# Two value products moved in the hand-written order of a two-layer graph-network kernel

## The chip, the cores and the metric

The kernel runs on one core of a Trainium2 chip. The metric is the device time of one execution in microseconds (us), as the median of several runs. A profile is one further execution, recorded by the hardware; its own time is given beside it. Engines are called by the profile's names: PE is the matmul engine and PEld its weight loads, DVE the vector engine, ACT the scalar engine, POOL the general engine, SP the engine that only issues DMAs here.

## The reference, cut to what matters

128 graphs of 128 nodes with 256 features each pass through two layers. The first is an attention layer whose attention matrix is split by edge type (four types, of which the adjacency here uses 0 and 1), followed by a norm, a feed-forward net with GELU and a second norm. The second consists of two graph attentions in a row, a norm, a feed-forward net with ReLU and a last norm.

```python
# layer 0
q, k = src @ Wq + bq, src @ Wk + bk                 # 8 heads of 32
attn = softmax(q k^T / sqrt(32))
out = sum over r of (attn * (adj == r)) @ (src @ Wv[r] + bv[r])
x = ln(src + out @ Wo + bo, g1, beta1)              # norm 0
x = ln(x + gelu(x @ W1 + b1) @ W2 + b2, g2, beta2)  # norm 1
# layer 1
h = gat(gat(x, adj, W1, a1), adj, W2, a2)
h = ln(x + h, g_ln1, b_ln1)                         # norm 2, "the graph norm"
x = ln(h + relu(h @ w_ff1 + b_ff1) @ w_ff2 + b_ff2, g_ln2, b_ln2)   # norm 3
```

All of it is float32. W1, W2, w_ff1 and w_ff2 are 256 x 1024 and 1024 x 256.

## The kernel before, in words

**Tiling.** The 16384 rows (128 graphs of 128 nodes) are worked in 32 groups of T = 512 rows, four graphs each. For each group the kernel keeps x (rows on partitions), xT (features on partitions) and the transposed adjacency. A second pass for general adjacencies exists behind a flag that the first pass computes; it doesn't run on these inputs.

**Steps as generators.** The work of a group is cut into Python generators, each `yield` being the end of a step: `projections` (two steps for q, two for k, then four for v, one for each block of 128 rows), `attention`, `norm`, `ffn`, `layer1`. The function `in_order` takes a list of such generators and calls the next step of each in the order of the list, with `(f2, 2)` for two steps in a row. That list, written by hand, fixes the order in which instructions stand in each engine's queue; nothing reorders them later. Waits between engines follow from the tiles that they share.

**The steady order.** From group 1 on (`g` in the loop over groups) one pass of the loop holds three groups at different stages: the first feed-forward net of S1 = group g + 1 (`f1`), the second one of S = group g (`f2`), the two graph attentions (`l1`), and the projections (`pr`), attention (`at`) and norm 0 of S2 = group g + 2. Two `in_order` lists make up the pass. The first ends in the transposes of S for its second feed-forward net (`turned(S, 2)`), the first half of the attention of S2 and the end of `f1`; the second begins with `f2`. `pr` has eight steps in the pass: four for q and k early in the first list, and four value products `pv` (L570), one for each block, around the point where the lists meet. Each value product is two 128x512 matmuls into one buffer of the PSUM pool `ps_s` (tag "s", four buffers in rotation, shared with score tiles, transposes and most other products), after which DVE adds the bias row into `v` (L574). In what follows they are called pv 0 to pv 3, and their sums v 0 to v 3. v 0 and v 1 are read by the first half of the attention, v 2 and v 3 by the second. The pass with g = 0 and the last ones have orders of their own, or no S2 left.

**The transposes.** `turned(S, 2)` transposes the four normalised blocks of x on PE (L290, tile `pt`, two tiles of four transposes), evicts them on ACT with the norm's scale and bias (L293, tile `yT`), and makes four sums of halves of yT on DVE (L378 to L381, tile `yS`). The blocks are normalised by ACT (L338, four instructions), which waits for a small DVE row `sh` (L333), which in turn waits for a power on POOL (L325), which waits for a DVE row (L324).

**The feed-forward nets.** Each is computed by a scheme of seven products of half-sized blocks instead of eight (Winograd's form of Strassen's). For each of four parts r of the hidden layer these products follow each other on PE (L400):

- P1, the form B11 with a11 (first step, `begun(0)`), into the bank `fa`; ACT copies it to the bank `seeded` (L438);
- P7, the form T3 with s3, into the bank `fe`; ACT copies it to `p7` (L445);
- the form T2 with s2, added into `seeded`; ACT copies the sum to `p16` (L449);
- B21 with a12, added into `fa`, then the activation on ACT (L424);
- T1 with s1, added into `seeded`; DVE adds p7 to the sum (L455), and ACT activates;
- T4 with a22, added into `fe`; DVE adds p16 (L459);
- P1 of the next part, and B22 with s4.

A second set of seven products (L409) makes the output.

**Around the change.** `n1` is the norm 1 of S1. It has been given its root (L324 and L325) at the end of the first list; its step in the second list is the normalisation itself (`sh` on DVE, four L338 on ACT). `n2` is the norm 2 of S; its two remaining steps are the multiplications and additions of rows on DVE (L356). `at` in the second list makes the score matmuls of the second half (L588, tiles `ps`, all four buffers of the pool) and their exponentials on ACT (L594). Ahead of it, `(at, 3)` in the first list has made the first half's sums (`pden` L615, `pav` L624), two copies on ACT (L632, L635), two reciprocals (L639, L641) and the products (L644) on DVE.

Of the kernel before, what the change touches and what calls it, by code (L numbers as in the profile page):

```python
# [106 lines left out]
def fast_pass(ctx, tc, a, out):  # L107
# [132 lines left out]
    def graph_weights():  # L240

        scr = cut(D)
        wa1 = k.columns(gw1, a1, scr, "1")
        wa2 = k.columns(gw2, a2, scr, "2")
        rhs = cut(NCH, D + 2)
        nc.vector.tensor_copy(rhs[:, :, :D], gw2)
        nc.vector.tensor_copy(rhs[:, :, D : D + 1], wa2[:, :, 1:2])
        nc.vector.tensor_copy(rhs[:, :, D + 1 : D + 2], wa2[:, :, 0:1])
        gw1T = cut(NCH, D)
        yield  # L250
        for m in range(NCH):
            pt = mm_tile(f"pgt_{m}")
            for c in range(NCH):
                nc.tensor.transpose(
                    pt[:, c * P : (c + 1) * P], gw1[:, c, m * P : (m + 1) * P], k.ident
                )
            nc.scalar.copy(gw1T[:, m, :], pt[:, :D])
        yield
        for m in range(NCH):
            pu = mm_tile(f"pgw_{m}")  # L260
            for c in range(NCH):
                nc.tensor.matmul(
                    pu[:, : D + 2], gw1T[:, c, m * P : (m + 1) * P], rhs[:, c, :],
                    start=(c == 0), stop=(c == NCH - 1),
                )
            nc.scalar.copy(wu[:, m, : D + 2], pu[:, : D + 2])
            nc.vector.tensor_copy(wu[:, m, D + 2 : D + 3], wa1[:, m, 1:2])
            nc.vector.tensor_copy(wu[:, m, D + 3 :], wa1[:, m, 0:1])
        yield
# [14 lines left out]
    def transposed(y, gc, bc, n):  # L284

        yT = w2p.tile([P, NCH, T], F32, tag="yT", name="yT_" + n)
        for c in range(NCH):
            pt = ps_s.tile([P, T], F32, tag="s", name=f"pt_{n}_{c}")
            for b in range(G):
                nc.tensor.transpose(  # L290
                    pt[:, b * P : (b + 1) * P], y[:, b, c * P : (c + 1) * P], k.ident
                )
            nc.scalar.activation(  # L293
                yT[:, c, :], pt, AF.Identity, bias=bc[:, c : c + 1], scale=gc[:, c : c + 1]
            )
        return yT
# [61 lines left out]
    def norm(S, i):  # L358

        root(S, i)  # L360
        yield
        normed(S, i)
        yield
        for step in range(2):
            scaled(S, i, step)
            yield
# [3 lines left out]
    def turned(S, i):  # L370
        n = f"{i}_{S['g']}"
        S["xT", i + 1] = yT = transposed(S["x"], *cols[i], n)
        if i == 1:
            return

        S["yS", i + 1] = ys = w1p.tile([P, 4, TH], F32, tag="yS", name="yS_" + n)
        a11, a21, a12, a22 = (yT[:, c, h * TH : (h + 1) * TH] for c in range(2) for h in range(2))
        nc.vector.tensor_sub(ys[:, 2], a11, a21)  # L378
        nc.vector.tensor_add(ys[:, 0], a21, a22)
        nc.vector.tensor_sub(ys[:, 1], a22, ys[:, 2])  # L380
        nc.vector.tensor_sub(ys[:, 3], a12, ys[:, 1])  # L381
# [170 lines left out]
    def projections(S):  # L552

        n, xt = str(S["g"]), S["xt"]
        for o, w, bias in (("qT", wq, bq), ("kT", wk, bk)):
            S[o] = w1p.tile([P, NCH, T], F32, tag=o, name=f"{o}_{n}")
            for m in range(NCH):
                pq = mm_tile(f"pq_{n}_{m}")
                for c in range(NCH):
                    nc.tensor.matmul(  # L560
                        pq, w[:, c, m * P : (m + 1) * P], xt[:, c, :],
                        start=(c == 0), stop=(c == NCH - 1),
                    )
                nc.scalar.activation(S[o][:, m, :], pq, AF.Identity, bias=bias[:, m : m + 1])
                yield
        for b in range(G):
            S["v", b] = v = w1p.tile([P, 2 * D], F32, tag=f"v{b}", name=f"v_{n}_{b}")
            pv = mm_tile(f"pv_{n}_{b}")
            for c in range(NCH):
                nc.tensor.matmul(  # L570
                    pv, xt[:, c, b * P : (b + 1) * P], wv[:, c].rearrange("p r d -> p (r d)"),
                    start=(c == 0), stop=(c == NCH - 1),
                )
            nc.vector.tensor_add(v, pv, bv)  # L574
            yield
# [198 lines left out]
    with tc.manual_schedule(engines={ET.PE, ET.Activation, ET.DVE, ET.SP, ET.Pool}):  # L774

        nc.tensor.matmul(seeded, k.ident, first["xt"][:, 0, :], start=True, stop=True)
        none = iter(())
        st = [first, second] + [None] * (NG - 2)
        S1 = st[1]
        gw, pr, at = graph_weights(), projections(first), attention(first)  # L780
        pr1, at1 = projections(S1), attention(S1)
        n0, n1_, n0_ = norm(first, 0), norm(first, 1), norm(S1, 0)
        prepared(first)
        in_order(
            lambda: combined(w1), (pr, 4), gw, (pr, 4), (at, 2), gw, at, lambda: combined(w2), at, gw, (at, 2), (pr1, 2), at,
            at, (pr1, 2), (at, 2), at, pr1, at, pr1, (n0, 2), lambda: turned(first, 0), (n0, 2),
        )
        f1 = first_ffn(first)
        prepared(S1)
        in_order(  # L790
            lambda: combined(u1), (f1, 4), at1, (f1, 4), at1, pr1, (f1, 3), (at1, 3), pr1, f1, at1, f1, at1,
            f1, f1, (at1, 3), f1, f1, at1, lambda: combined(u2), f1, at1, f1, n0_, f1, n0_, (f1, 2), lambda: turned(S1, 0), n1_, (n0_, 2),
        )
        for g in range(NG - 1):
            S, S1 = st[g], st[g + 1]
            more = g + 2 < NG
            f1, f2 = first_ffn(S1), second_ffn(S)
            n1, n2 = norm(S1, 1), norm(S, 2)
            pr = at = n0 = none
            if more:  # L800
                S2 = st[g + 2] = entered(g + 2)
                pr, at, n0 = projections(S2), attention(S2), norm(S2, 0)
            ready = (lambda: prepared(S2)) if more else (lambda: None)
            if g == 0:
                in_order((f1, 2), n1_, pr, (f1, 2), lambda: turned(S, 1), (n1_, 2))
                l1 = layer1(S)
                in_order(
                    f1, l1, f1, l1, f1, l1, (f1, 2), pr, (f1, 4), pr, f1, (l1, 3), f1, pr, f1, l1, f1,
                    l1, pr, f1, pr, f1, (l1, 3), f1, pr, f1, l1, n2, (at, 2), f1, n2, f1, n1, pr,
                    lambda: turned(S, 2), (at, 3),  # L810
                )
            else:
                n3 = norm(st[g - 1], 3)
                in_order(
                    pr, lambda: turned(S1, 0), pr, f1, f2_, n3, f1, n0_, (f1, 4), n0_, (f1, 2), n3, l1, f1, f1, l1, n3,
                    (f1, 3), pr, n3, lambda: store(st[g - 1]), f1, f1, exp, l1, l1, pr, f1, l1, f1,
                    f1, l1, n2, f1, at, n2, at, f1, pr, lambda: turned(S, 2), pr, (at, 3), f1, f1, pr, n1,
                )
            if not more:
                break  # L820
            l1 = layer1(S1)
            in_order(
                f2, pr, f2, n1, (n2, 2), f2, at, (f2, 2), lambda: turned(S1, 1), (f2, 2), at, (n1, 2),
                (f2, 2), l1, at, ready, (f2, 4), l1, f2, at, f2, l1, (f2, 2), at, at, f2, at, n0, l1, f2,
                n0, l1, gelu, f2, l1, f2,
            )
            n0_, f2_ = n0, f2
        in_order((f2, 2), n1, (f2, 2), lambda: turned(S1, 1), (n2, 2))
        l1 = layer1(S1)
        in_order(  # L830
            f2, (l1, 2), f2, l1, (n1, 2), (f2, 8), (l1, 3), f2, l1, f2, l1, (f2, 4), (l1, 3), f2, l1,
        )
        n2, n3 = norm(S1, 2), norm(S, 3)
        in_order(n2, f2, n2, (f2, 2), lambda: turned(S1, 2))
        f2 = second_ffn(S1)
        in_order((f2, 14), (n2, 2), (n3, 4), lambda: store(S), (f2, 2))
        checks()
        in_order((f2, 4))
        for p in (1, 0):
            root(S1, 3, pair(p))  # L840
            normed(S1, 3, pair(p))
            for step in range(2):
                scaled(S1, 3, step, (p,))
            store(S1, pair(p))
            if p == 1:
                in_order((f2, 2))
# [345 lines left out]
```

## Time and profile before

| what | value |
|---|---|
| runs | 2836.33, 2838.88, 2835.97 us (median 2836.33) |
| the profiled run | 2840.0 us, span 2837.9 us |
| granted clock of PE | 0.991 of full |
| PE, PEld, DVE, ACT, POOL busy | 2776.8, 2233.8, 2176.8, 1568.5, 162.2 us |
| one pass of the steady loop (1016.70 to 1102.40 us): PE, DVE, ACT busy | 85.57, 67.42, 48.77 us of 85.70 |
| value products L570 | 512 matmuls, 597 ns each, 242.3 us |
| their additions L574 | 128, 682 ns each (median) |
| normalisations L338 | 384, 597 ns each; ACT idle before them 180.5 us |

Matmuls overlap each other in the record, and the recorded end of a matmul is modelled: what a group of matmuls takes is better read from the distance between its start and the start of the next group. A value product of two float32 matmuls stands as four records of 128x512, as every float32 matmul here (transposes apart) stands as two. The busy time of DVE and ACT can be read as it stands.

### The profile page before, as it was taken

How to read it: one execution, taken by the hardware profiler on the slowest of the kernel's cores; microseconds unless marked ns; L12 is line 12 of the kernel's file. 1: busy time of each engine (PE TensorE's matmuls, PEld its weight loads, DVE VectorE, ACT ScalarE, POOL GpSimd, SP SyncE). 2: the span in 40 equal slices, each digit the busy share in tenths (PEclk: the TensorE clock that was granted, in tenths of full speed). 3: DMA queues.
4: the chain of work that ended last, by engine and by line, in shares of the span. 5: the costliest groups of instructions: out<-in, count | busy, mean ns of one | idle time of the engine just before them, and what ended most of it. 6: DMA issues, size and time to landing. Idle time of an engine off the chain costs nothing.

```text
span 2837.9 us, 51798 instructions
## 1 busy us (share of the span) xinstructions
PE 2776.8 (98%) x20816; PEld 2233.8 (79%) x20816; DVE 2176.8 (77%) x5068; ACT 1568.5 (55%) x3395; POOL 162.2 (6%) x153
## 2 busy tenths in 40 slices
PE   8999999999999999999999999999999999999986
PEld 4778788887888887888887887887887887888875
DVE  6677887877787877777877777778778778878765
ACT  3545555556555556555556565556556555555552
POOL 3000000000000000000000000000000000000000
PEclk9999999999999999999999999999999999999998
DMA  6010110010111010111010111000110001110000
GB/s 173 5 27 15 32 35 34 24 34 12 34 35 34 23 35 12 35 34 34 23 35 12 35 34 34 24 26 21 34 35 27 31 15 32 35 34 23 16 16 20
DMA packets 70645, 87.27 MB, mean 31 GB/s; under 512 B 8192, under 2 KB 48512, under 8 KB 70400
## 3 DMA queue, kind: packets, MB, share of 16 engines
q1 hardware_dynamic: 69568, 83.52, 9.5%
q8 instruction: 164, 2.69, 0.4%
q14 instruction: 81, 0.66, 0.1%
q10 hardware_dynamic: 832, 0.40, 0.0%
HBM read 66.99 MB, written 16.91 MB: 30 GB/s over the span
## 4 chain that ended last, share of the span: by engine, by line
PE 86%; ACT 7%; DVE 2%; issue 0%; POOL 0%; POOLq 0%; DVEq 0%; ACTq 0%
PE ph L400 14%; PE po L409 14%; PE seeded L409 12%; PE seeded L400 11%; PE pq L560 7%; PE pv L570 6%; PE pw L713 4%; PE pav L624 4%; ACT x L338 4%; PE pwo L662 4%; PE pt L290 3%; PE pden L615 2%; PE py L726 2%; PE pg L738 2%; ACT e L594 1%; PE ps L588 1%
## 5 line engine op out<-in xcount | busy, mean ns | idle before, releaser
L338 ACT ACTIVATE x<-x,sh,rs 128x256 f32<-128x256 f32 x384 | 199.4, 597 | 180.5 <-DVE sh L333 180.5
L325 POOL TENSOR_TENSOR rs<-rs,mhalf 128x4 f32<-128x4 f32 x129 | 138.8, 1076 | 2635.0 <-DVE rs L324 2225.5
L594 ACT ACTIVATE e<-ps 128x512 f32<-128x512 f32 x256 | 131.8, 601 | 209.1 <-PE ps L588 209.1
L570 PE MATMUL pv<-wv,xT 128*128 128x512 f32 x512 | 242.3, 597 | 0.3 <-ACT e L594 0.3
L400 PE MATMUL seeded<-yS,w_L_gnn_w_ff 128*128 128x256 f32 x768 | 207.3, 392 | 5.0 <-ACT seeded L472 1.3
L400 PE MATMUL seeded<-yS,w_L_gnn_W 128*128 128x256 f32 x768 | 204.0, 388 | 2.4 <-ACT seeded L472 1.3
L455 DVE TENSOR_TENSOR hT<-seeded,p 128x512 f32<-128x512 f32 x128 | 88.5, 692 | 148.3 <-PE seeded L400 148.3
L400 PE MATMUL ph<-yT,w_L_gnn_w_ff 128*128 128x256 f32 x768 | 199.0, 388 | 0.0
L310 DVE BATCH_NORM_STATS2 st<-x 128x6 f32<-128x256 f32 x512 | 192.5, 418 | 7.7
L400 PE MATMUL ph<-yT,w_L_gnn_W 128*128 128x256 f32 x768 | 194.4, 382 | 2.4 <-ACT yT L293 2.4
L409 PE MATMUL po<-w_L_gnn_W,hT 128*128 128x128 f32 x1536 | 190.1, 277 | 0.0
L409 PE MATMUL po<-w_L_gnn_w_ff,hT 128*128 128x128 f32 x1536 | 187.0, 275 | 0.0
L409 PEld LDWEIGHTS po<-w_L_gnn_w_ff,hT 128*128 128x128 f32 x1536 | 184.0, 192 | 3.2
L409 PEld LDWEIGHTS po<-w_L_gnn_W,hT 128*128 128x128 f32 x1536 | 181.7, 192 | 5.7 <-issue 0.5
L400 PEld LDWEIGHTS seeded<-yS,w_L_gnn_W 128*128 128x128 f32 x768 | 138.4, 190 | 52.7 <-issue 15.6
L400 PEld LDWEIGHTS seeded<-yS,w_L_gnn_w_ff 128*128 128x128 f32 x768 | 137.8, 190 | 48.9 <-ACT p L449 24.6
L400 PEld LDWEIGHTS ph<-yT,w_L_gnn_W 128*128 128x128 f32 x768 | 144.2, 191 | 38.0 <-ACT yT L293 10.2
L400 PEld LDWEIGHTS ph<-yT,w_L_gnn_w_ff 128*128 128x128 f32 x768 | 139.2, 191 | 38.3 <-issue 13.9
L602 DVE TENSOR_TENSOR pm<-e,adj 128x512 f32<-128x512 f32 x256 | 161.7, 693 | 4.1 <-ACT e L594 4.1
L686 ACT ACTIVATE gs<-spread,wh 128x128 f32<-128x128 f32 x128 | 40.9, 390 | 187.1 <-DMA spread<-hbm 187.1
L424 ACT ACTIVATE hT<-hT,c_L_gnn_b 128x256 f32<-128x256 f32 x256 | 109.4, 497 | 61.4 <-DVE hT L455 60.3
L570 PEld LDWEIGHTS pv<-wv,xT 128*128 128x128 f32 x512 | 90.7, 192 | 66.1 <-issue 63.6
(155 smaller groups left out, 6116.4 us busy)
## 6 DMA issues: line engine op xcount, KB each, us to landing
xT<-in_xT_dram SPq DMA_DIRECT2D x32, 512.0 KB, 7.1
x<-in_x_dram SPq DMA_DIRECT2D x32, 512.0 KB, 8.3
spread<-hbm SPq DMA_DIRECT2D x64, 256.0 KB, 4.2
out_dram<-x SPq DMA_DIRECT2D x31, 512.0 KB, 2.9
adj<-in_adjT_dram SPq DMA_DIRECT2D x32, 256.0 KB, 6.0
w_L_gnn_W<-in_L_gnn_W_dram SPq DMA_DIRECT2D x8, 256.0 KB, 7.3
w_L_gnn_w_ff<-in_L_gnn_w_ff_dram SPq DMA_DIRECT2D x8, 256.0 KB, 5.1
hbm<-line SPq DMA_DIRECT2D x64, 2.0 KB
```

The lines of the kernel that those rows point to most:

```text
L310: nc.vector.bn_stats(st[:, b % 2, :], S["x"][:, b, :])
L325: nc.gpsimd.tensor_tensor(rs[:, bs], rs[:, bs], k.mhalf[:, bs], op=ALU.pow)
L338: nc.scalar.activation(x[:, b, :], x[:, b, :], AF.Identity, bias=sh[:, b : b + 1], scale=rs[:, b : b + 1],)
L400: nc.tensor.matmul(bank[:, s * TH : (s + 1) * TH], wa[:, form, 0, f * P : (f + 1) * P], m, start=start and s == 0, stop=True, skip_group_c ...
L409: nc.tensor.matmul(bank[:, s * P : (s + 1) * P], m[:, f, s * P : (s + 1) * P], wb_[:, form, f, :], start=start and s + f == 0, stop=True, ...
L560: nc.tensor.matmul(pq, w[:, c, m * P : (m + 1) * P], xt[:, c, :], start=(c == 0), stop=(c == NCH - 1),)
L570: nc.tensor.matmul(pv, xt[:, c, b * P : (b + 1) * P], wv[:, c].rearrange("p r d -> p (r d)"), start=(c == 0), stop=(c == NCH - 1),)
L594: nc.scalar.activation(e[:, s], pss[s], AF.Exp, scale=SCALE)
L602: nc.vector.tensor_mul(pm[:, s], S["e", p][:, s], S["ad"][:, pair(p), None, :].to_broadcast([P, 2, NCH, P]),)
L624: nc.tensor.matmul(pav[s * DH : (s + 1) * DH, u, c, :], v[:, d0 : d0 + DH], m[:, s, u, c, :], start=(r == 0), stop=(r == 1),)
L662: nc.tensor.matmul(po[:, s * D : (s + 1) * D], oT[:, c, b * P : (b + 1) * P], wo[:, c, :], start=(c == 0), stop=(c == NCH - 1),)
L713: nc.tensor.matmul(pw[:, :NU], yT[:, c, b * P : (b + 1) * P], wu[:, c, :], start=(c == 0), stop=(c == NCH - 1),)
```

## The change

Both edits are in the two lists of the steady order.

```diff
-    f1, l1, n2, f1, at, n2, at, f1, pr, lambda: turned(S, 2), pr, (at, 3), f1, f1, pr, n1,
+    f1, l1, n2, f1, at, n2, at, f1, pr, pr, lambda: turned(S, 2), (at, 3), f1, f1, pr, n1,
...
-    f2, pr, f2, n1, (n2, 2), f2, at, (f2, 2), lambda: turned(S1, 1), (f2, 2), at, (n1, 2),
+    (f2, 2), n1, pr, (n2, 2), f2, at, (f2, 2), lambda: turned(S1, 1), (f2, 2), at, (n1, 2),
```

In the first list pv 1 now stands ahead of the eight transposes of `turned(S, 2)`; before it stood behind them, so that both pv 0 and pv 1 are now ahead. In the second list pv 3 now stands behind P7 of the second feed-forward net and behind n1's normalisation; before it stood between P1 and P7.

On the engines, in each pass with g = 1 to 29: PE's order changes at these two places. On DVE, v 1 now stands ahead of the four yS instructions, and `sh` of n1 (L333) ahead of v 3. The order on ACT, POOL and SP is the same, and no instruction is added or removed. Since the pool `ps_s` hands out its buffers in the order of the list, the rotation changes with it: the first tile of transposes takes the third buffer after the scores' own instead of the second, and so on; pden takes pv 0's buffer in both orders, and the fourth score tile of the second half takes pv 3's.

## The prediction

> **What bounds the kernel now.** I read the page's busy shares and chain first, then the table of waits, then the timeline of one steady iteration (from 1013 to 1036.5 us), row by row, on all engines.
>
> ```profile
> PE 2776.8 (98%) x20816; PEld 2233.8 (79%) x20816; DVE 2176.8 (77%) x5068; ACT 1568.5 (55%) x3395; POOL 162.2 (6%) x153
> ...
> PE 86%; ACT 7%; DVE 2%; issue 0%; POOL 0%; POOLq 0%; DVEq 0%; ACTq 0%
> ```
>
> PE holds 86% of the chain that ended last, ACT 7%. A matmul's end is modelled, so 98% busy says little; I measure loss by the distance between starts. The row of pv at 1014.96 stands at 1100.68 one iteration later, and its transposes at 245.11 and 2645.56 at the two ends of the run, 28 iterations apart: 85.73 us each, all alike. What is saved once is saved 29 times (g = 1 to 29).
>
> ```profile
> 1014.96 1.88 PE L570 MATMUL pv<-wv,xT 128*128 128x512 f32 x4
> 1015.08 2.08 ACT L338 ACTIVATE x<-x,sh,rs 128x256 f32<-128x256 f32 x4
> 1016.68 1.30 PE L290 MATMUL pt<-ident,x 128*128 128x128 f32 x8
> 1017.21 0.53 PEld L290 LDWEIGHTS pt<-ident,x 128*128 128x128 f32 x5 [0.28 <-ACT x L338]
> 1017.81 1.88 PE L570 MATMUL pv<-wv,xT 128*128 128x512 f32 x4
> ```
>
> First place. Columns: start, duration, engine, line, operands, count, idle before and its releaser. The four normalisations on ACT end at 1017.16, the transposes reach PE at 1016.68; the fourth waits. From 1016.68 to 1017.81 is 1.13 us for eight transposes; the same eight at 1033.67 take 0.87. Loss 0.26.
>
> ```profile
> 1025.97 1.03 PE L400 MATMUL ph<-yT,w_L_gnn_w_ff 128*128 128x256 f32 x4
> 1026.84 1.88 PE L570 MATMUL pv<-wv,xT 128*128 128x512 f32 x4
> 1028.56 1.03 PE L400 MATMUL ph<-yS,w_L_gnn_w_ff 128*128 128x256 f32 x4
> 1028.76 0.69 DVE L574 TENSOR_TENSOR v<-pv,r_L_gnn_bv 128x512 f32<-128x512 f32 x1 [1.32 <-PE pv L570]
> 1029.36 0.15 DVE L333 SCALAR_TENSOR_TENSOR sh<-mv,rs 128x4 f32<-128x4 f32 x1
> 1029.62 0.59 ACT L445 COPY p<-ph 128x512 f32<-128x512 f32 x1 [2.01 <-PE ph L400]
> 1030.10 2.08 ACT L338 ACTIVATE x<-x,sh,rs 128x256 f32<-128x256 f32 x4
> 1031.48 1.13 PE L400 MATMUL ph<-yT,w_L_gnn_w_ff 128*128 128x256 f32 x4
> 1032.08 0.57 ACT L449 COPY p<-seeded 128x512 f32<-128x512 f32 x1
> 1032.70 0.73 PEld L400 LDWEIGHTS seeded<-yS,w_L_gnn_w_ff 128*128 128x128 f32 x4 [0.49 <-ACT p L449]
> 1032.70 1.13 PE L400 MATMUL seeded<-yS,w_L_gnn_w_ff 128*128 128x256 f32 x4
> ```
>
> Second place. Read down: P1 (B11), pv of block 3, P7, later B21 at 1031.48 and T1 at 1032.70. ACT has nothing for 2.01 us, then must do p7, four normalisations and p16 in a row; T1 overwrites seeded, so it waits until p16 has been copied. B21 to T1 is 1.22 us; such a product takes 0.86 (1028.56 to 1029.42). Of the 0.36 lost, 0.11 belongs to the change from 32-row score matmuls to 128 rows (the po group after scores takes 1.89, others 1.78), so 0.25 is the wait. T1 then takes 0.97 (to 1033.67), another 0.11.
>
> ```profile
> 1034.54 1.75 PE L400 MATMUL ph<-yT,w_L_gnn_w_ff 128*128 128x256 f32 x7
> 1035.37 0.73 PEld L400 LDWEIGHTS ph<-yT,w_L_gnn_w_ff 128*128 128x128 f32 x4 [0.21 <-ACT hT L424]
> ```
>
> Third: T4 and the next B11 take 1.80 (to 1036.34) instead of 1.72, 0.08 lost on ACT's activation, which stands behind the same ACT block. The rest of the iteration has no such wait on PE, only steps of about 0.1 at changes of tile shape or after short waits.
>
> **What the Trainium skill says.** "TensorE: Matmul & The Clock Gate", section "Step-by-step: what each phase is for", says that PE pulls only weight loads ahead and keeps matmuls in program order: one late operand stops all behind it. The trace agrees (T1's loads idle 0.49, everything waits). Its section "LDWEIGHTS (loading the stationary operand)" gives P/1.2 ns, an estimate of 107 ns for 128 columns, for a load that can't be hidden; after the wait T1 takes 0.11 us more: agrees. "Perfetto Trace Analysis", section "Tensor Engine Instruction (MATMUL, LD_WEIGHTS)", calls ACT and DVE strict FIFO: so the order of sh and the v addition on DVE counts. The rows above stand in program order.
>
> **The change, part by part.** Nothing is added or removed: per iteration two pv products (four 128x512 matmuls in all) and their DVE additions change place, and n1's normalisation now stands ahead of pv 3 on DVE. POOL's and SP's orders are the same; ACT's order is the same too. No DMA is issued by a moved step. SP's load of the next xT waits for pv 3, its last reader, so it and what is queued behind it on SP may go 0.6 us later (0.86 of P7, less 0.26); xT's next use is at 1065.03, 36 us on, against a median 7.1 us to land: hidden.
>
> *pv 1 ahead of the transposes.* pv 0 to 1016.68, pv 1 to 1018.40; ACT's normalisations ended at 1017.16, so the transposes run 1018.40 to 1019.27 unhindered. Gain 0.26. The switch to pden (0.09 over pv's 1.72 before) remains. Pool "s" has four buffers: pden takes pv 0's, free when v 0 is added at 1018.82. The yT evictions, before 1017.58 to 1019.02, now lie at 1019.09 to 1020.54; yS on DVE follows, its last starting at about 1021.4 instead of 1019.86, so the first reciprocal starts near 1021.73 instead of 1021.48. DVE is solid from there to the L324 row: 0.25 later, at 1027.53. ACT's rd is not later (pden ends 0.26 earlier).
>
> *pv 3 behind P7.* On PE's new clock (0.26 earlier): P1 1025.71, P7 1026.57, pv 3 1027.44, T2 1029.15, scores 1030.11. p7 is copied at about 1027.6 in ACT's idle stretch. sh needs POOL: L324 ends 1027.69, POOL starts 0.17 later and takes 1.01, some 0.1 to DVE (not shown alone; 0 to 0.27 by the row at 1014.35 after a POOL end of 1014.08): sh at 1028.97, where before it stood behind v 3 at 1029.36. Normalisations start at 1029.17 instead of 1030.10, p16 is done at 1031.72. T1 is due at 1030.11 + 1.10 (scores) + 0.97 (B21 with its switch) = 1032.18: no wait. Gain 0.25 + 0.11, and 0.08 at the third place, as ACT's block is 0.93 earlier and PE 0.62.
>
> *The new wait.* Behind sh on DVE stands v 3, behind that the g and b rows of L356 (2.5 us, used some 20 us later) and hT L455. The fourth score tile takes pv 3's buffer and needs v 3: added 0.20 after pv 3's issue, 1029.35 to 1030.04; PE asks at 1030.13. A DVE end reaches PE 0.055 us later in the final rows (2831.090 to 2831.145). So 0.03 us to spare: cost 0, bounded by below nothing (no path) and 0.2 above. All queues behind it move together with PE, and hT L455 is due at 1033.3, DVE free at 1032.5.
>
> **Sum.** 0.26 + 0.25 + 0.11 + 0.08 = 0.70 us, times 29 = 20.3. The profiled span is 2837.9, its run 2840.0; runs lie at 2835.97 to 2838.88. From the median 2836.33: 2816.
>
> **Rivals.**
> *Part of it* (2820 to 2829): the 0.03 is missed by 0.1 to 0.2, or the first or second place keeps a wait; only the first gain gives 2828.6. For it: the margin is thinner than POOL's spans are exact. Against: even then 0.5 of 0.70 remains.
> *Nothing* (2833 to 2840): ACT's block does not start earlier, since sh comes 0.9 late, and T1 waits as long as before; the time of the first place is then lost at the second. Against: DVE's row is counted through. That the change does not do what it says is excluded: the order of instructions shows both moves in g = 1 to 29.
> *Slower* (about 2846): sh is late by more. Once it comes after 1029.35 (0.38 later than worked out), v 3 and the scores wait for it one to one, and PE, which never waited for POOL here, does. At 1.08 late the gain is gone; at 1.4 late, 0.32 us x 29 = 9 us are lost. For it: yS and two long reciprocals stand in front of sh on DVE, and yS is later. Against: only 0.25 of lateness can be found.
>
> **How the numbers follow.** All of it 0.68 (2813 to 2819; steps of 0.1 at shape changes make 3 us either way), part 0.20, nothing 0.05, slower 0.07. Range 2812 to 2827 holds the first and most of the second. Faster by over 0.2% (5.7 us, about what a measurement of this kernel can tell from no change): 0.88; within 0.05; slower 0.07.
>
> **What would show it.** Period 85.03 instead of 85.73. pt at L290 behind two pv, eight transposes in 0.87 with no ACT L338 before them; p7's copy before sh; B21 to T1 0.97, T1 0.86; sh ahead of v 3. Wrong if the first scores' weight loads idle on DVE v L574, or POOL rs L325 stands among PE's or DVE's long waits.

## The result and the profile after

| kernel | median, us | range | runs |
|---|---|---|---|
| before | 2837.61 | 2835.97 to 2839.44 | 4 |
| changed | 2815.83 | 2812.69 to 2819.03 | 4 |

The ratio is 0.9923 with a 95% interval of 0.9906 to 0.994: 0.77% faster, 21.8 us between the medians. The profiled execution of the changed kernel has a span of 2815.3 us; before it was 2837.9.

The page of the changed kernel, busy shares and chain:

```profile
PE 2757.6 (98%) x20816; PEld 2240.4 (80%) x20816; DVE 2181.7 (77%) x5068; ACT 1575.5 (56%) x3395; POOL 162.3 (6%) x153
...
PE 92%; DVE 2%; ACT 1%; issue 0%; POOL 0%; POOLq 0%; DVEq 0%; ACTq 0%
```

The busy shares hardly tell the two kernels apart. The chain does: ACT's part fell from 7% to 1%, and PE's rose from 86% to 92%. In four steady passes of the kernel before (those that start near 1014, 1099, 1527 and 2042 us) the chain steps over to ACT at one or both of the two places; in the same part of the changed kernel's run it does not.

The timeline of one steady pass of the changed kernel, the two places in turn (start, duration, engine, line, operands, count, idle before and its releaser). These rows lie 6.83 us earlier in the span than the same pass of the kernel before.

```profile
1008.13 3.60 PE L570 MATMUL pv<-wv,xT 128*128 128x512 f32 x8
1008.26 2.08 ACT L338 ACTIVATE x<-x,sh,rs 128x256 f32<-128x256 f32 x4
1011.57 1.04 PE L290 MATMUL pt<-ident,x 128*128 128x128 f32 x8
1012.53 1.06 PE L615 MATMUL pden<-e,ones 128*32 128x512 f32 x8
```

The last row in the kernel before:

```profile
1019.62 1.06 PE L615 MATMUL pden<-e,ones 128*32 128x512 f32 x8
```

First place: two value products run from 1008.13, and the normalisations end at 1010.34, more than a microsecond before the transposes. From 1011.57 to 1012.53 is 0.96 us: 0.87 for the transposes and 0.09 for the switch to pden's 32 columns, which before stood behind pv 1 (the split is taken over from there: pv 1 with the switch took 1.81, a value product without it 1.72). From pv 0 to pden it is 4.40 us; before it was 4.66 (1014.96 to 1019.62).

```profile
1018.88 1.03 PE L400 MATMUL ph<-yT,w_L_gnn_w_ff 128*128 128x256 f32 x4
1019.75 1.03 PE L400 MATMUL ph<-yS,w_L_gnn_w_ff 128*128 128x256 f32 x4
1020.61 1.88 PE L570 MATMUL pv<-wv,xT 128*128 128x512 f32 x4
1020.81 0.59 ACT L445 COPY p<-ph 128x512 f32<-128x512 f32 x1 [0.29 <-PE ph L400]
1021.99 0.16 DVE L333 SCALAR_TENSOR_TENSOR sh<-mv,rs 128x4 f32<-128x4 f32 x1 [1.21 <-POOL rs L325]
1022.19 2.08 ACT L338 ACTIVATE x<-x,sh,rs 128x256 f32<-128x256 f32 x4 [0.79 <-DVE sh L333]
1022.53 0.69 DVE L574 TENSOR_TENSOR v<-pv,r_L_gnn_bv 128x512 f32<-128x512 f32 x1 [0.38 <-PE pv L570]
1023.28 1.17 PE L588 MATMUL ps<-qT,kT 32*128 32x128 f32 x32
1024.17 0.56 ACT L449 COPY p<-seeded 128x512 f32<-128x512 f32 x1
1024.39 1.13 PE L400 MATMUL ph<-yT,w_L_gnn_w_ff 128*128 128x256 f32 x4
1025.14 0.84 PEld L400 LDWEIGHTS seeded<-yS,w_L_gnn_w_ff 128*128 128x128 f32 x4
1025.36 1.03 PE L400 MATMUL seeded<-yS,w_L_gnn_w_ff 128*128 128x256 f32 x4
1027.09 1.89 PE L400 MATMUL ph<-yT,w_L_gnn_w_ff 128*128 128x256 f32 x8
```

Second place: P1, P7, pv 3 in the new order. p7's copy falls into ACT's idle stretch; sh now waits for POOL, not behind v 3. T1's weight loads no longer idle for ACT: they start 0.22 ahead of T1, where before both started at 1032.70, after the wait. B21 (1024.39) to T1 (1025.36) is 0.97, T1 to the transposes at 1026.22 is 0.86, and T4 with the next P1 (1027.09 to 1028.82) is 1.73. The period, from pv at 1008.13 to pv at 1093.16, is 85.03 us.

### The profile page after: what moved, and what is told of

It is laid out like the page before. It is cut to its first block, busy times and chain, and to the rows that moved or that the text cites. A ratio compares the mean times of both kernels' runs of the same rounds, so it can differ in the third digit from the quotient of the medians.

```text
span 2815.3 us, 51827 instructions
## 1 busy us (share of the span) xinstructions
PE 2757.6 (98%) x20816; PEld 2240.4 (80%) x20816; DVE 2181.7 (77%) x5068; ACT 1575.5 (56%) x3395; POOL 162.3 (6%) x153
## 4 chain that ended last, share of the span: by engine, by line
PE 92%; DVE 2%; ACT 1%; issue 0%; POOL 0%; POOLq 0%; DVEq 0%; ACTq 0%
PE po L409 16%; PE ph L400 15%; PE seeded L400 12%; PE seeded L409 12%; PE pq L560 7%; PE pv L570 7%; PE pw L713 4%; PE pav L624 4%; PE pwo L662 4%; PE pt L290 3%; PE ps L588 2%; PE pden L615 2%; PE py L726 2%; PE pg L738 2%; ACT x L338 0%; DVE st L310 0%
## 5 line engine op out<-in xcount | busy, mean ns | idle before, releaser
L570 PE MATMUL pv<-wv,xT 128*128 128x512 f32 x512 | 235.7, 593 | 0.5 <-ACT e L594 0.5
```

The source lines that it names most:

```text
L570: nc.tensor.matmul(pv, xt[:, c, b * P : (b + 1) * P], wv[:, c].rearrange("p r d -> p (r d)"), start=(c == 0), stop=(c == NCH - 1),)
```

## The experiments

Seven kernels were timed, each against the kernel before on the same chip: the first four together (before: 2836.17 us, median of 20 runs), the last three together (before: 2835.5 us, 17 runs). The ratio is that to the kernel before, with its 95% interval in brackets. "Period" is the distance between the starts of the same row of PE in two steady passes; it repeats to 0.01 us within a trace, so it separates what the times alone could not.

### The first edit alone

```diff
-    ..., pr, lambda: turned(S, 2), pr, (at, 3), ...
+    ..., pr, pr, lambda: turned(S, 2), (at, 3), ...
```

> Only the first edit: pv 1 ahead of the eight transposes; pv 3 and n1 as in the kernel before. Theory (two separate waits of PE, the second one set by PE itself through P7 and p7's copy): the 0.26 us of the transposes are saved and kept, since P7, p7's copy and the four normalisations all come 0.26 earlier; T1's wait of 0.25 stays. Period 85.46 us, 29 x 0.26 = 7.7 us less than before. Rival (the normalisations, and with them T1, are set by DVE's row sh, which this edit makes 0.25 later): what is saved at the transposes is waited for again at T1, period 85.7, no change.

Measured: 2828.65 us, ratio 0.9973 (0.9962 to 0.9983), 7.5 us less than before; period 85.46. Its timeline at the second place:

```profile
1028.07 2.08 ACT L338 ACTIVATE x<-x,sh,rs 128x256 f32<-128x256 f32 x4
1029.45 1.13 PE L400 MATMUL ph<-yT,w_L_gnn_w_ff 128*128 128x256 f32 x4
1030.66 0.73 PEld L400 LDWEIGHTS seeded<-yS,w_L_gnn_w_ff 128*128 128x128 f32 x4 [0.49 <-ACT p L449]
```

T1's weight loads idle for 0.49 as before, no more and no less. The wait at the second place moves along with PE: what the transposes save is kept. The rival falls: sh still stands behind v 3 and starts 0.61 after it, as before (0.60).

### The second edit alone

```diff
-    f2, pr, f2, n1, (n2, 2), f2, at, ...
+    (f2, 2), n1, pr, (n2, 2), f2, at, ...
```

> Only the second edit: pv 3 behind P7 and behind n1's normalisation; the transposes stand between pv 0 and pv 1 as before. Theory: the wait of T1 (0.25), the unhidden weight load after it (0.11) and the wait of the next B11 (0.08) go, the transposes keep their 0.26. Period 85.29 us, 29 x 0.44 = 12.8 us less than before. Rival (the two places share one slack, so that either edit alone brings nearly all): period near 85.05 us, 20 us less.

Measured: 2824.43 us, ratio 0.996 (0.9946 to 0.9973), 11.7 us less; period 85.30. The two savings per pass, 0.27 of the first edit and 0.43 of this one, add up to the 0.70 of the whole change: the two places are independent. The rival falls.

### The second edit without the earlier norm

```diff
-    (f2, 2), n1, pr, (n2, 2), f2, at, ...
+    (f2, 2), pr, n1, (n2, 2), f2, at, ...
```

> As the changed kernel, but n1's normalisation stays behind pv 3: P1, P7, pv 3, n1. Theory (what counts is when sh is made on DVE): sh stands behind v 3 again, which now comes 0.86 later, so the normalisations start about 0.9 us later than they could, p16 ends about 0.57 after T1 is due; with the unhidden weight load 0.11 and the next B11 0.08 the period is 85.8 us, nothing left of the gain, about 2 us slower than before. Rival (what counts is PE's order, P7 ahead of pv 3, since p7's copy then fills ACT's idle stretch): period stays near 85.05 us, 20 us less than before.

Measured: 2838.14 us, ratio 1.0006 (0.9997 to 1.0014): by the times, not to be told from the kernel before. By the period, 85.78, it is 0.05 us a pass slower than that, and 0.75 slower than the changed kernel. Its timeline:

```profile
1029.58 0.69 DVE L574 TENSOR_TENSOR v<-pv,r_L_gnn_bv 128x512 f32<-128x512 f32 x1 [1.76 <-PE pv L570]
1030.19 0.15 DVE L333 SCALAR_TENSOR_TENSOR sh<-mv,rs 128x4 f32<-128x4 f32 x1
1030.38 2.08 ACT L338 ACTIVATE x<-x,sh,rs 128x256 f32<-128x256 f32 x4 [1.93 <-DVE sh L333]
1032.97 0.73 PEld L400 LDWEIGHTS seeded<-yS,w_L_gnn_w_ff 128*128 128x128 f32 x4 [0.81 <-ACT p L449]
```

sh stands behind v 3, v 3 waits 1.76 us for the later pv 3, and ACT idles 1.93 us for sh with POOL's part long done (POOL ended at 1029.00 in this pass). T1's loads idle 0.81. The first edit is in this kernel too, so pv 3's new place alone is judged against the first edit alone: 85.78 against 85.46, a loss of 0.32 us a pass, which uses up what the first edit saves.

### The earlier norm without moving the product

```diff
-    (f2, 2), n1, pr, (n2, 2), f2, at, ...
+    f2, n1, pr, f2, (n2, 2), f2, at, ...
```

> As the changed kernel, but pv 3 stays between P1 and P7, with n1's normalisation in front of it: P1, n1, pv 3, P7. ACT now makes the four normalisations ahead of p7's copy. Theory (sh's time counts, PE's order of pv 3 and P7 does not): the normalisations run from 1.3 us after P7's old place in the queue, p7 and p16 follow and p16 ends about 0.1 us before T1 is due; only the next B11 may wait 0.02 to 0.1. Period 85.03 to 85.15 us, 17 to 20 us less than before. Rival (P7 ahead of pv 3 is needed to fill ACT's idle stretch): T1 waits again, period 85.4 us or more, at most 10 us less.

Measured: 2821.72 us, ratio 0.995 (0.9936 to 0.9963), 14.4 us less than before; period 85.11. By the period 29 x 0.62 = 18.0 us are saved, within the interval and in the expected range; the median alone is 2.5 us short of that range. All its five runs had a mean granted clock of 0.991 or 0.992, while half of the runs of the kernel before had 0.993, and a lower clock goes with a longer time (last section). Among the runs at 0.991 alone the medians differ by 15.6 us, still short of the range. Its timeline:

```profile
1022.49 0.16 DVE L333 SCALAR_TENSOR_TENSOR sh<-mv,rs 128x4 f32<-128x4 f32 x1 [1.21 <-POOL rs L325]
1022.57 0.68 DVE L574 TENSOR_TENSOR v<-pv,r_L_gnn_bv 128x512 f32<-128x512 f32 x1
1022.69 2.08 ACT L338 ACTIVATE x<-x,sh,rs 128x256 f32<-128x256 f32 x4 [1.66 <-DVE sh L333]
1024.67 0.56 ACT L445 COPY p<-ph 128x512 f32<-128x512 f32 x1
1025.13 0.58 ACT L449 COPY p<-seeded 128x512 f32<-128x512 f32 x1
1025.87 1.03 PE L400 MATMUL seeded<-yS,w_L_gnn_w_ff 128*128 128x256 f32 x4
```

p7's copy comes after the normalisations now, p16 ends at 1025.71 and T1 starts at 1025.87 without a wait. Only the next P1 waits 0.08 again, since ACT's block ends half a microsecond later. So most of what the second edit brings, 0.35 of 0.43 by the periods (85.46 to 85.11 to 85.03), comes from sh standing ahead of v 3. The place of pv 3 behind P7 is worth the remaining 0.08, and only with the norm in front. The rival falls: P7 need not go first for T1's wait to vanish.

### v 3 added later

```diff
-    (f2, 2), n1, pr, (n2, 2), f2, at, ...
+    (f2, 2), n1, n2, pr, n2, f2, at, ...
```

> As the changed kernel, but one step of n2 (two row multiplications on DVE, 0.60 us each from start to start) stands between sh and v 3 instead of behind v 3. No work is added. Theory (the fourth score tile needs the buffer that v 3 frees, with less than 0.1 us to spare): v 3 is added about 0.7 us later, the first scores wait for it 0.7 us, ACT's block is not touched. Period 85.75 us, all of the gain lost, about 2837 us. Rival (the scores do not wait for v 3 in earnest, the buffer is free in time): period 85.03, 20 us less than before.

Measured: 2836.87 us, ratio 1.0003 (0.9995 to 1.0011); period 85.73. Its timeline at the scores:

```profile
1027.47 1.29 DVE L356 TENSOR_TENSOR x<-x,r_L_gnn_g_ln 128x512 f32<-128x512 f32 x2
1028.68 0.68 DVE L574 TENSOR_TENSOR v<-pv,r_L_gnn_bv 128x512 f32<-128x512 f32 x1
1028.70 0.50 PE L588 MATMUL ps<-qT,kT 32*128 32x128 f32 x6
1029.42 0.76 PEld L588 LDWEIGHTS ps<-qT,kT 32*128 32x128 f32 x24 [0.42 <-DVE v L574]
```

The first matmuls of three score tiles run from 1028.70 (six records), the fourth tile waits for v 3, added 1028.68 to 1029.36, and PE goes on at 1029.42. The group of scores takes 1.80 us instead of 1.10. A row step of DVE that nobody needs for 20 us costs 0.70 us a pass from where it stands, the whole gain. The last link of the rival "slower", from v 3 to the scores, is real, and its price is one to one: against the scores' first row v 3 comes 0.73 later than in the changed kernel and costs 0.70, so the room there was some 0.03 (an estimate, 0.73 less 0.70). A late sh ahead of v 3 was not tried.

### One more step moved, and the change again

In the changed kernel the second part of the same feed-forward net still has a short wait of the same kind. The step of pden and pav can stand between T2 and B21.

```diff
-    (f2, 2), l1, at, ready, (f2, 4), l1, f2, at, f2, l1, ...
+    (f2, 2), l1, f2, at, ready, (f2, 3), l1, f2, at, f2, l1, ...
```

> The changed kernel with one more step moved: in the second part of the second feed-forward net, T2 goes ahead of the second half's sums (pden, pav), which so lie between T2 and B21. In the changed kernel T1 of that part waits 0.03 us for p16 and then pays 0.105 us for a weight load that is not hidden; with 2.7 us of sums between them, p16 is long done. Theory (PE is the bound, each such 0.1 us counts in full): period 84.90 us, 30 x 0.135 = 4 us less than the changed kernel. Rival (the sums come 0.96 us later, and the reciprocals on DVE behind them then hold up the output projection, or T2 waits for its own copy): no change against the changed kernel, or some us slower.

> The changed kernel itself, beside the two others of this call on the same chip: period 85.03 us, about 20 us less than before.

Measured: 2813.61 us with the step moved (2813.07 to 2813.63; ratio to before 0.992, 0.9906 to 0.9933), 2818.02 for the change again (2814.89 to 2819.2; ratio 0.9934, 0.9921 to 0.9948). Periods 84.89 and 85.03, 0.13 us apart before rounding; over 30 passes that is 4.0 us, and 4.4 lie between the medians. The median of the change again is only 17.5 us less than before, where 20 were expected. Three of its five runs had a granted clock of 0.991, and nine of the 17 of the kernel before had 0.993; between runs of equal clock the medians differ by 20.2 us (0.991) and 20.0 (0.993). The same place, first in the changed kernel, then with the step moved:

```profile
1035.14 1.13 PE L400 MATMUL seeded<-yS,w_L_gnn_w_ff 128*128 128x256 f32 x4
1036.10 1.03 PE L400 MATMUL ph<-yT,w_L_gnn_w_ff 128*128 128x256 f32 x4
1036.36 0.59 ACT L449 COPY p<-seeded 128x512 f32<-128x512 f32 x1 [1.47 <-PE seeded L400]
1037.00 0.73 PEld L400 LDWEIGHTS seeded<-yS,w_L_gnn_w_ff 128*128 128x128 f32 x4 [0.27 <-ACT p L449]
```

```profile
1029.44 1.03 PE L400 MATMUL seeded<-yS,w_L_gnn_w_ff 128*128 128x256 f32 x4
1030.56 0.59 ACT L449 COPY p<-seeded 128x512 f32<-128x512 f32 x1 [0.54 <-PE seeded L400]
1033.14 1.13 PE L400 MATMUL ph<-yT,w_L_gnn_w_ff 128*128 128x256 f32 x4
1034.11 1.03 PE L400 MATMUL seeded<-yS,w_L_gnn_w_ff 128*128 128x256 f32 x4
```

p16 ends at 1031.15, three microseconds before T1 at 1034.11, and T1's loads no longer wait for ACT. The rival falls: the period shows no new loss from the later sums. This version is the fastest of all that were run; its margin over the change rests on the period, since single runs nearly meet here and one run of the changed kernel in its first timing was shorter (2812.69).

## Why the prediction was right

The forecast was 2816.0 us, 20.3 less than before; measured were 2815.83 and 21.8 less. That the median came within 0.2 us is luck, since runs of the changed kernel spread over 6.3 us. The period is not: it was to be 85.03 and is 85.03, and the sum holds term by term. Of the 22.6 us between the two profiled spans, 29 x 0.70 = 20.3 is the loop, the rest lies ahead of it and behind it.

| term, us a pass | forecast | trace after |
|---|---|---|
| wait of the fourth transpose | 0.26 | 0.26 (pv 0 to pden 4.40, was 4.66) |
| T1's wait for p16 | 0.25 | 0.25 (B21 to T1 0.97, was 1.22) |
| T1's first weight load, not hidden | 0.11 | 0.11 (T1 0.86, was 0.97) |
| next P1's wait for the activation | 0.08 | 0.07 (1.73, was 1.80) |

The steps behind the terms, on the clock of the kernel before (add 6.83 to the rows after):

| step | forecast | trace after |
|---|---|---|
| first reciprocal on DVE (L639 at 1014.83 after) | 1021.73 | 1021.66 |
| sh | 1028.97 | 1028.82 |
| normalisations | 1029.17 | 1029.02 |
| v 3 | 1029.35 | 1029.36 |
| scores | 1030.11 | 1030.11 |
| T1 | 1032.18 | 1032.19 |

The step with the widest bounds was POOL's hand-over to DVE, put at 0.1 us: POOL's row starts at 1020.95 and takes 1.01, sh starts at 1021.99, so it is 0.03. That made sh 0.15 earlier than forecast, together with a reciprocal that started 0.07 earlier; neither is on the path, since v 3 waits for pv 3 (DVE idles 0.38 between sh and v 3). The prediction's 0.38 of room for sh left out the 0.08 that sh takes before v 3 can start (1022.49 to 1022.57 in the kernel with the earlier norm alone); by its own times the room was 0.30, by the trace 0.46.

One of the prediction's two signs of being wrong came true all the same. The scores' weight loads don't idle for v 3 in the steady passes, but POOL does stand among DVE's long waits:

```profile
DVE sh L333 <- POOL rs L325: 37.8, 32, 1.2
```

The columns are us in total, number of waits and the longest: some 1.2 us in each pass, where before there were three such waits in the whole run, 2.7 us in all. The sign was badly chosen. The prediction's own times leave DVE idle for 1.28 us between L324 and sh, and this idling takes the place of the 1.32 us that v 3 waited before. It delays nothing that PE waits for.

The rivals. "Part of it" did not come about: the new wait of the scores has so little room that v 3, added until 1023.22, and the scores' first row at 1023.28 are 0.06 apart, and yet it costs nothing. "Nothing" needed ACT's block to stay where it was; the experiment without the earlier norm starts the normalisations 0.04 after the scores, where they stood 0.28 ahead of them before and 1.09 in the changed kernel, and the gain is gone. "Slower" named the right place: delaying v 3 by 0.7 us costs 0.70. The change misses that loss because it puts nothing between sh and v 3, and sh comes early enough. The forecast treated the second edit as one; the experiments show that its two halves are unequal, with pv 3's new place a loss of 0.32 alone and worth 0.08 with the norm in front.

## What to carry to other kernels

In a loop whose main engine has no slack, read the distance between starts of its groups against the same group elsewhere in the loop: a tenth that one takes longer was here a wait, an unhidden load or a change of tile shape. The change of shape stayed wherever the group was put; each wait and load that was taken away counted in full, once a pass. A small row operation that another engine waits for goes ahead of a larger one whose own operand comes late, because in an in-order queue it otherwise waits for that operand too (ACT idled 1.93 us for sh in the kernel without the earlier norm, 0.79 in the changed one); and when a product is moved later, look for who needs the buffer that its consumer frees.

## What was not expected of the hardware

The four runs of the changed kernel spread over 6.3 us (2812.69 to 2819.03), though the period of its two traces is the same 85.03. The difference between these two traces, 2815.3 and 2813.2 us, lies in the end of the program. Windows near the end, first of the one, then of the other (window, length, busy time and count of PE, PEld, DVE, ACT and POOL, granted clock of PE, DMA share, GB/s):

```profile
2700.00:2720.00 20.00, 17.41 (x95) 14.13 (x94) 12.73 (x37) 9.85 (x19) 2.02 (x2) 0.91 0.00 0
2720.00:2740.00 20.00, 15.08 (x71) 12.20 (x71) 11.12 (x26) 10.86 (x27) 0.00 (x0) 0.90 0.04 14
```

```profile
2700.00:2720.00 20.00, 16.85 (x100) 13.42 (x99) 12.62 (x36) 10.46 (x20) 2.01 (x2) 1.00 0.00 0
2720.00:2740.00 20.00, 15.08 (x69) 12.09 (x69) 11.13 (x26) 10.89 (x27) 0.00 (x0) 0.93 0.04 14
```

There PE is no longer busy throughout, and its granted clock falls below 1.00 at places that differ from run to run; in three steady passes of the kernel before, early, in the middle and late, it was 1.00. The mean clock of each run goes with its time: of the kernel before, the ten runs at 0.993 beside the first four experiments took 2833.07 to 2836.03 us, the six at 0.990 or 0.991 took 2836.97 to 2839.11; of the changed kernel, all nine runs counted, four at 0.993 took 2812.69 to 2815.13 and five at 0.991 took 2817.26 to 2819.2. That the lower clock makes the whole difference was not tried. The traces do show that spans differ by a microsecond or two without any difference in the loop, so that small changes here are better told by the period.
